# A graph-layer kernel on one core: the running sums of two batches overlapped, five tables instead of four, set-up issued in another order, and a new list of step times

## The chip, the core and the metric

The kernel runs on one core of one Trainium2 chip. The metric is the device time in microseconds (us) of one execution. Before the change three runs took 2403.47, 2404.86 and 2407.35 us, a median of 2404.86 us.

The engines have short names in the profile: PE is TensorE (matmuls; PEld is its weight load), DVE is VectorE, ACT is ScalarE, POOL is GpSimd, SP is SyncE, which here only issues transfers. Each of them takes its instructions in the order in which the program lists them.

## The reference

`x` holds 32 batches of 512 channels by 1024 nodes, `adj` is 512 by 512. There are two layers, each a normalisation over the nodes, a relu, and a graph operation that is added to `x`:

```python
# layer 0: attention over the nodes
h = relu(layernorm(x))
q, k = einsum('c,bcn->bn', wq, h), einsum('c,bcn->bn', wk, h)
scores = q[:, None, :] + k[:, :, None]
scores = where(scores > 0, scores, 0.01 * scores)
att = softmax(scores, axis=-1)                    # 1024 x 1024 a batch
agg = einsum('bcn,bmn->bcm', h, att)
x = x + relu(einsum('oc,bcm->bom', adj, agg) + bm[None, :, None])
# layer 1: a product with the squared adjacency
h = relu(layernorm(x))
x = x + einsum('bnf,nm->bmf', h, adj * adj) + bias
```

A score depends on one number of the row and one of the column. So the attention needs no 1024 by 1024 matrix: with the nodes sorted by `q`, each output row is a combination of a prefix sum and a suffix sum of the sorted value rows, read at the row where the sign of the score changes.

## The kernel before

**What a batch passes through.** The functions below are the steps of one batch, in the order of the data; PE's instructions for each are given.

- `load` brings the four 128 by 1024 pieces of `x` in, `stats` (DVE), `norm` (ACT: square root), `slopes` (DVE) and `relu` (ACT) make `h` from them. Layer 0 and layer 1 use the same functions (`stats0`, `stats1` and so on in the list of times).
- `scores` makes `q` and `k` on PE (tile `pq`), copies them out on ACT (`qr`), and sends them through memory (`qd`) into a row on all partitions, `qrow`. `columns` turns them into columns (`pr`, `qk`).
- `value` makes the 1024 value rows, eight tiles `pv` of eight matmul instructions; `spread` copies each to SBUF on ACT (tile `v`).
- `rank` counts on DVE how many `q` are smaller (eight columns of nodes); `lower` finds on ACT where the score changes sign. `to_rows`, `factors` and `from_rows` turn both into row numbers and factors on DVE.
- `scatter` writes the value rows on POOL's queue to their sorted places in a table in DRAM, `td`. There are `TABLES` of these, used in turn by the batches.
- `fetch` reads the sorted rows back (tiles `vs`, three a batch, from a pool of five), `weights` (ACT), `later` (DVE), `totals` (PE, tile `pd`) and `stationary` (POOL, tile `sm`) make the triangular matrices for the sums.
- `scan` is a chain of nine links. Each multiplies one block of the prefix sum and one of the suffix sum, 64 columns each (PE, tile `sc`, four instructions). `sums` copies its last row on ACT into the first row of the next block (L522, L523), so that the next link can start, then copies the block (L525, L526) and sends it to the table.
- `gather` reads each node's row of sums with eight indirect transfers on POOL's queue (tile `g`), `excess` and `divide` (DVE, with an exponential on ACT), `weigh` (ACT) and `combine` (DVE) put them together, and `turn` transposes the result on PE (tile `tr`) and adds it on DVE to a second copy of `x`, which `reload` brought (tiles `y`).
- `propagate` is layer 1's product: eight tiles `pg` of eight matmul instructions. `finish` (DVE) adds it and sends a piece of the output.

**What sets the order.** Nothing is scheduled by need. `PLAN` gives each step a time within its batch. Batch `b` adds `b * T`; the first and the last five batches are shifted by `FIRST` and `LAST`. All steps are sorted by that time and issued in that order:

```python
for n, t in enumerate(times):
    t = s.b * T + t + shift + stretch * (t - mean)
    steps.append((t, len(steps), f, (s, *lead, *(args[n] if args else (n,)))))
```

So the times are only an order, one for all engines; what an engine does at a moment follows from its own list and from its waits. PE's eight PSUM banks (`bank`) are handed out in the order of release. A tile that finds its bank still in use makes PE wait for the ACT or DVE instruction that empties it.

**One period.** In the middle of the run PE's list for a period is `scores` of batch b, its eight `value` tiles, the nine links of batch b-1, the eight `propagate` tiles of b-3 and the `turn` of b-2. Nearly every link stands alone between two tiles of 512 columns.

**Set-up.** Ahead of all steps the adjacency is loaded on SP's queue, then vectors on ACT's queue, masks are made on POOL and DVE, sixteen transfers of `pad` rows go out on ACT's queue (L260, L261), the adjacency is transposed on PE (L267) and copied by DVE (L268), and squared on POOL.

Of the kernel before, what the change touches and what calls it, by code (L numbers as in the profile page):

```python
# [16 lines left out]
P = 128  # L17
# [8 lines left out]
TABLES = 4  # L26
PLAN = {
    "columns": (1.84,),
    "combine": (
        214.04, 217.22, 206.24, 213.22, 203.06, 204.85, 202.37, 208.83, 220.2,  # L30
        221.83, 210.28, 216.32, 220.61, 221.9, 203.97, 206.56,
    ),
    "divide": (197.69,),
    "excess": (192.58,),
    "factors": (26.85,),
    "fetch": (67.06,),
    "finish": (275.07, 275.57, 281.48, 295.03, 317.93, 325.21, 315.57, 329.77),
    "from_rows": (68.15,),
    "gather": (160.21, 160.88, 169.39, 162.65, 163, 180.52, 164.85, 177.34),
    "later": (80.96,),  # L40
    "lift": (262.58, 269.88, 268.88, 273.93),
    "load": (-129.22, -82.94, -100.13, -53.61),
    "lower": (19.51, 17.67, 17.14, 24.76, 5.02, 13.05, 20.96, 48.33),
    "norm0": (-19.68,),
    "norm1": (240.99,),
    "propagate": (259.13, 265.4, 277.44, 283.36, 299.38, 300.5, 305.97, 309.52),
    "rank": (10.11, 17.8, 19.14, 5.65, 29.55, 35.11, 29.97, 33.03),
    "reload": (206.53, 195.2, 186.44, 204.89),
    "relu0": (-13.28, -12.83, -12.78, -11.68),
    "relu1": (248.39, 248.69, 248.95, 251.18),  # L50
    "scan": (86.07, 89.94, 103.3, 112.5, 121.08, 133.74, 140.67, 149.41, 151.56),
    "scatter": (40.11, 33.33, 32.57, 31.18, 51.68, 50.03, 50.02, 50.12),
    "scores": (-3.28,),
    "slopes0": (-19.05,),
    "slopes1": (244.13,),
    "spread": (14.21, 19.99, 13.53, 9.98, 24.66, 40.56, 35.96, 32.13),
    "stationary": (82.64, 96.64, 117.94),
    "stats0": (-76.58, -67.19, -75.23, -31.79),
    "stats1": (234.63, 235.11, 239.07, 234.96),
    "sums": (86.61, 100.16, 109.91, 113.65, 123.33, 138.82, 142.68, 150.09, 152.34),  # L60
    "to_rows": (27.23, 39.48),
    "totals": (84.47,),
    "turn0": (224.81, 225, 224.25, 224.65),
    "turn1": (229.2, 229.61, 229.06, 228.65),
    "value": (1.31, 6.43, 2.58, -2.04, 12.64, 17.61, 9.29, 13.53),
    "weigh": (211.43, 203.12, 199.8, 199.59, 214.55, 207.84, 213.35, 199.85),
    "weights": (77.29,),
}
FIRST = {
    "columns": ((10.25, 0), (-8.88, 0), (-1.28, 0), (-0.35, 0), (-4.55, 0)),  # L70
    "combine": ((0.76, -0.179), (2.86, -0.007), (1.11, -0.052), (2.15, 0.315), (3.85, -0.295)),
    "divide": ((-2.63, 0), (-3.76, 0), (1.77, 0), (-5.55, 0), (5.22, 0)),
    "excess": ((-1.4, 0), (-1.74, 0), (0.78, 0), (-1.88, 0), (-0.04, 0)),
    "factors": ((-1.65, 0), (0.24, 0), (-11.11, 0), (20.41, 0), (5.22, 0)),
    "fetch": ((1.66, 0), (1.42, 0), (0.16, 0), (2.7, 0), (2.46, 0)),
    "finish": ((7.67, -0.035), (-1.07, -0.048), (-1.08, -0.19), (1.65, 0.072), (7.11, -0.138)),
    "from_rows": ((-7.36, 0), (5.32, 0), (0.41, 0), (-11.13, 0), (1.83, 0)),
    "gather": ((2.03, -0.347), (6.25, 0.095), (6.91, -0.157), (4.86, 0.109), (-0.48, -0.141)),
    "later": ((0.59, 0), (-0.89, 0), (0.46, 0), (-1.56, 0), (-1.25, 0)),
    "lift": ((2.63, 0.053), (-2.39, -0.028), (-8.8, -0.373), (4.29, -0.574), (-5.63, -0.61)),  # L80
    "load": ((-4.06, 0.422), (-19.27, 0.242), (-9.74, -0.1), (-43.08, -0.218), (3.83, -0.041)),
    "lower": ((10.06, 0.047), (-2.11, 0.029), (0, 0.006), (-1.47, -0.638), (-0.64, -0.541)),
    "norm0": ((-0.28, 0), (-7, 0), (-16.93, 0), (-5.48, 0), (-7.56, 0)),
    "norm1": ((-2.89, 0), (-2.28, 0), (5.13, 0), (-4.22, 0), (4.28, 0)),
    "propagate": ((-0.51, -0.089), (-2.12, 0.048), (-0.37, -0.024), (0.9, -0.087), (0.8, -0.134)),
    "rank": ((12.28, 0.08), (-2.69, 0.063), (-1.25, -0.191), (-2.72, -0.187), (3.67, 0.356)),
    "reload": ((13.1, -0.159), (1.05, 0.07), (0.55, -0.006), (5.79, -0.056), (6.93, 0.28)),
    "relu0": ((4.04, -0.722), (-9.03, 0.1), (0.87, 0.055), (-1.74, 0.026), (-4.5, -0.079)),
    "relu1": ((-6.02, -0.262), (3.93, 0.189), (0.12, 0.08), (-6.68, -0.3), (5.36, -0.097)),
    "scan": ((-3.08, 0.008), (0.76, 0.008), (0.29, 0.01), (4.39, 0.049), (0.02, 0.004)),  # L90
    "scatter": ((9.9, -0.497), (-2.67, -0.18), (-1.41, -0.166), (13.52, 0.471), (-0.96, -0.009)),
    "scores": ((11.05, 0), (-7.18, 0), (-1.43, 0), (-1.1, 0), (-5.18, 0)),
    "slopes0": ((5.94, 0), (-4.02, 0), (-4.68, 0), (-4.91, 0), (-5.3, 0)),
    "slopes1": ((-4.88, 0), (-3.92, 0), (2.98, 0), (-6.44, 0), (6.4, 0)),
    "spread": ((15.49, -0.014), (-8.28, 0.055), (-1.18, 0.339), (5.11, -0.246), (-4.18, -0.13)),
    "stationary": ((-0.45, 0.012), (-3.58, -0.066), (2.3, 0.037), (3.72, 0.043), (0.11, 0.066)),
    "stats0": ((-4.41, 0.092), (-1.09, -0.037), (-11.92, -0.19), (-11.74, 0.144), (-4.6, 0.06)),
    "stats1": ((-4.42, -0.05), (-0.78, -0.165), (-2.4, -0.195), (-1.72, -0.801), (-0.4, -0.191)),
    "sums": ((-1.59, 0.008), (1.44, 0.008), (0.8, 0.011), (4.47, 0.048), (0.33, 0.004)),
    "to_rows": ((10.45, -0.184), (-1.39, -0.051), (-3.95, 0.188), (-5.12, -0.008), (3.22, 0.411)),  # L100
    "totals": ((-0.39, 0), (-1.31, 0), (2.21, 0), (3.78, 0), (-0.88, 0)),
    "turn0": ((-2.67, -0.147), (0.79, 0.144), (0.98, 0.006), (-1.5, -0.73), (2.76, -0.161)),
    "turn1": ((-5.71, 0.295), (-0.45, 0.083), (1.67, -0.222), (0.23, -0.077), (1.24, 1.019)),
    "value": ((12.84, -0.049), (-4.18, -0.108), (-0.34, -0.035), (-1.68, 0.56), (-0.83, -0.076)),
    "weigh": ((3.71, -0.151), (-4.8, 0.011), (2.02, 0.13), (-3.07, 0.09), (4.7, 0.116)),
    "weights": ((3.98, 0), (-0.18, 0), (3.93, 0), (-5.45, 0), (-0.47, 0)),
}
LAST = {
    "columns": ((-0.38, 0), (3.24, 0), (0.03, 0), (-4.32, 0), (-5.95, 0)),
    "combine": ((-13.52, -0.583), (-7.79, -0.661), (2.57, 0.018), (5.39, 0.14), (1.5, -0.058)),  # L110
    "divide": ((-17.36, 0), (-2.76, 0), (-0.77, 0), (1.72, 0), (-5.29, 0)),
    "excess": ((-15.23, 0), (-5.2, 0), (-2.78, 0), (5.24, 0), (-2.45, 0)),
    "factors": ((-2.1, 0), (-19.01, 0), (38.03, 0), (-13.91, 0), (0.21, 0)),
    "fetch": ((3.7, 0), (-1.79, 0), (-2.6, 0), (2.41, 0), (-10.36, 0)),
    "finish": ((37.02, -0.24), (-20.28, -0.179), (-0.12, 0.054), (7.26, 0), (7.17, 0.076)),
    "from_rows": ((-5.28, 0), (-0.46, 0), (19.09, 0), (10.28, 0), (-5.76, 0)),
    "gather": ((-7.27, -0.089), (-1.57, 0.275), (14.67, -0.488), (6.08, 0.503), (-1.65, 0.527)),
    "later": ((-2.82, 0), (-3.64, 0), (-2.12, 0), (1.08, 0), (-9.77, 0)),
    "lift": ((-33.59, -0.326), (-26.78, 0.49), (-1.54, 0.547), (5.74, 0.408), (-8.25, -0.218)),
    "load": ((0.07, 0.087), (2.75, -0.35), (4.99, -0.213), (-6.16, 0.111), (-0.4, -0.03)),  # L120
    "lower": ((-2.66, -0.306), (11.93, 0.06), (2.85, -0.242), (9.18, -0.176), (-3.11, 0.105)),
    "norm0": ((-8.11, 0), (-9.42, 0), (-8.14, 0), (-18.6, 0), (-2.96, 0)),
    "norm1": ((-25.17, 0), (-15.22, 0), (8.43, 0), (4.77, 0), (3.62, 0)),
    "propagate": (
        (-30.65, -0.512), (-18.28, -0.071), (-2.12, -0.017), (6.79, -0.024), (0.98, -0.118),
    ),
    "rank": ((-1.62, -0.025), (0.93, -0.001), (1.88, -0.179), (-4.5, 0.134), (-5.28, 0.009)),
    "reload": ((-20.37, -0.165), (5.3, 0.015), (4.48, 0.302), (2.59, -0.107), (7.99, -0.179)),
    "relu0": ((-0.04, 0.046), (3.05, 0), (1.47, -0.143), (-0.13, -0.026), (-2.37, 0.467)),
    "relu1": ((-21.92, -0.142), (-17.67, -0.206), (5.39, -0.385), (9.69, 0.26), (1.51, 0.12)),  # L130
# [22 lines left out]
def kernel(  # L153
# [104 lines left out]
    for td in tds:  # L258
        for o in range(2):
            nc.scalar.dma_start(sorted_rows(td, 0, NB)[o, 0], pad[0:NB, :])  # L260
            nc.scalar.dma_start(sorted_rows(td, NB - 1, 1)[o, :, 0], pad[0:HP, :])  # L261
# [401 lines left out]
```

## Time and profile before

| what | value |
|---|---|
| runs | 2403.47, 2404.86, 2407.35 us |
| the profiled execution | 2408.7 us, of it the span of instructions 2406.7 us |
| busy: PE, DVE, ACT, POOL | 2330.6, 1930.8, 1589.9, 687.6 us |
| share of the span: PE, DVE, ACT, POOL | 97%, 80%, 66%, 29% |
| transfers | 643.17 MB, mean 267 GB/s |
| mean granted clock of TensorE | 0.987 |

A page of the profile comes from one execution. Busy time is the time in which an engine executed; matmuls are pipelined, so that the mean duration of one (602 ns) is longer than the distance between two. A row of the timeline gives the start, the length and, in brackets, how long the engine had been idle and what ended that. The slices of the page cut the span in 40 equal parts.

### The profile page before, as it was taken

How to read it: one execution, taken by the hardware profiler on the slowest of the kernel's cores; microseconds unless marked ns; L12 is line 12 of the kernel's file. 1: busy time of each engine (PE TensorE's matmuls, PEld its weight loads, DVE VectorE, ACT ScalarE, POOL GpSimd, SP SyncE). 2: the span in 40 equal slices, each digit the busy share in tenths (PEclk: the TensorE clock that was granted, in tenths of full speed). 3: DMA queues.
4: the chain of work that ended last, by engine and by line, in shares of the span. 5: the costliest groups of instructions: out<-in, count | busy, mean ns of one | idle time of the engine just before them, and what ended most of it. 6: DMA issues, size and time to landing. Idle time of an engine off the chain costs nothing.

```text
span 2406.7 us, 28301 instructions
## 1 busy us (share of the span) xinstructions
PE 2330.6 (97%) x7632; PEld 981.1 (41%) x7632; DVE 1930.8 (80%) x5012; ACT 1589.9 (66%) x2873; POOL 687.6 (29%) x973
## 2 busy tenths in 40 slices
PE   6889999999999999999999999999999999999898
PEld 2233444443444444444444444444344444444333
DVE  6568788888888898888898888888888878787765
ACT  3667667577676677667677667677767666757551
POOL 1233233223222223322323322323323223323310
PEclk9889999999999999999999999999999999999999
DMA  5689889898888898899898899889889888788882
GB/s 169 176 280 288 273 261 313 250 278 294 272 296 282 248 293 288 270 294 286 258 274 292 275 284 292 270 259 293 282 280 295 238 263 288 260 283 267 263 268 95
DMA packets 206718, 643.17 MB, mean 267 GB/s; under 512 B 29080, under 2 KB 29208, under 8 KB 206560
## 3 DMA queue, kind: packets, MB, share of 16 engines
q1 hardware_dynamic: 146704, 370.65, 54.5%
q0 software_dynamic: 57344, 268.99, 29.2%
q10 hardware_dynamic: 2512, 1.73, 0.3%
q8 instruction: 62, 1.02, 0.2%
q14 instruction: 96, 0.79, 0.1%
HBM read 429.94 MB, written 211.32 MB: 266 GB/s over the span
## 4 chain that ended last, share of the span: by engine, by line
PE 82%; DMA 5%; DVE 5%; ACT 3%; issue 2%; POOL 1%; SPq 1%; ACTq 0%; POOLq 0%; DVEq 0%
PE pg L577 33%; PE pv L429 31%; PE sc L512 11%; PE tr L570 4%; PE pq L326 2%; DMA vs<-td 1%; DMA td<-v,idx 1%; DMA qd<-qr 1%; DVE junk L371 1%; DVE st L296 1%; DVE g L563 1%; DMA qrow<-qd 1%; DVE junk L366 1%; ACT g L559 1%; POOL td L442 1%
## 5 line engine op out<-in xcount | busy, mean ns | idle before, releaser
L577 PE MATMUL pg<-h,wsq 128*128 128x512 f32 x2048 | 937.1, 602 | 7.7 <-ACT h L314 7.7
L429 PE MATMUL pv<-wmT,x 128*128 128x512 f32 x2048 | 910.8, 598 | 0.8 <-DVE y L585 0.8
L577 PEld LDWEIGHTS pg<-h,wsq 128*128 128x128 f32 x2048 | 374.4, 191 | 525.7 <-issue 495.2
L429 PEld LDWEIGHTS pv<-wmT,x 128*128 128x128 f32 x2048 | 379.8, 190 | 493.4 <-issue 458.3
L534 POOL DMA_INDIRECT g<-td,idg x256 | 247.7, 967 | 755.2 <-DMA qd<-qr 248.2
L442 POOL DMA_INDIRECT td<-v,idx x256 | 272.1, 1063 | 572.6 <-ACT vs L523 208.2
L522 ACT COPY vs<-sc 1x512 f32<-1x512 f32 x256 | 146.0, 570 | 388.4 <-PE sc L512 375.9
L512 PE MATMUL sc<-vs,sm 128*64 128x512 f32 x1152 | 332.2, 629 | 28.3 <-ACT vs L522 17.2
L382 ACT ACTIVATE junk<-qrow,qk 128x1024 bf16<-128x1024 f32 x256 | 294.0, 1148 | 91.6 <-DVE qk L345 47.6
L563 DVE SCALAR_TENSOR_TENSOR g<-g,cf 128x512 f32<-128x512 f32 x512 | 348.3, 742 | 4.9 <-ACT g L559 4.6
L585 DVE SCALAR_TENSOR_TENSOR y<-pg,bm_sb,y 128x512 f32<-128x512 f32 x256 | 186.0, 738 | 77.1 <-PE pg L577 75.6
L572 DVE SCALAR_TENSOR_TENSOR y<-tr,nbm,y 128x512 f32<-128x512 f32 x256 | 176.9, 744 | 62.1 <-PE tr L570 57.8
L525 ACT COPY t<-sc 128x512 f32<-128x512 f32 x288 | 168.8, 586 | 84.0 <-PE sc L512 65.8
L371 DVE TENSOR_SCALAR_CACHE_REDUCE junk<-qrow,qk,cnt 128x640 bf16<-128x640 f32 (+6 forms) x224 | 180.4, 805 | 8.2
L366 DVE TENSOR_SCALAR_CACHE_REDUCE junk<-qrow,qk 128x384 bf16<-128x384 f32 (+6 forms) x224 | 165.2, 737 | 19.6 <-DMA qrow<-qd 12.2
L559 ACT ACTIVATE g<-g,cf 128x512 f32<-128x512 f32 x256 | 169.6, 717 | 3.1 <-DVE cf L553 2.9
L296 DVE BATCH_NORM_STATS2 st<-x 128x6 f32<-128x512 f32 x256 | 162.7, 676 | 0.0
L296 DVE BATCH_NORM_STATS2 st<-y 128x6 f32<-128x512 f32 x256 | 160.2, 668 | 0.0
L320 DVE TENSOR_TENSOR y<-y,bias_sb 128x1024 f32<-128x1024 f32 x128 | 155.6, 1225 | 5.6 <-ACT h L314 5.5
L436 ACT COPY v<-pv 128x512 f32<-128x512 f32 x256 | 144.3, 578 | 20.1 <-PE pv L429 13.8
L314 ACT ACTIVATE x<-x,nmr,rstd 128x1024 f32<-128x1024 f32 x128 | 148.5, 1232 | 9.6 <-DVE nmr L307 9.6
L512 PEld LDWEIGHTS sc<-vs,sm 128*64 128x64 f32 x1152 | 63.7, 137 | 220.2 <-issue 96.7
(107 smaller groups left out, 1815.5 us busy)
## 6 DMA issues: line engine op xcount, KB each, us to landing
vs<-td SPq DMA_DIRECT2D x192, 384.8 KB
td<-t SPq DMA_DIRECT2D x576, 128.2 KB
x<-in_x_dram SPq DMA_DIRECT2D x128, 512.0 KB
y<-in_x_dram SPq DMA_DIRECT2D x128, 512.0 KB
out_dram<-y SPq DMA_DIRECT2D x128, 512.0 KB
qrow<-qd SPq DMA_DIRECT2D x32, 512.0 KB
td<-v,idx POOLq DMA_INDIRECT x256
g<-td,idg POOLq DMA_INDIRECT x256
```

The lines of the kernel that those rows point to most:

```text
L296: nc.vector.bn_stats(st[:, i, :], s.x[c][:, ts(i, HALF)])
L366: nc.vector.tensor_scalar(junk[:, 0 : j * P], s.qrow[:, 0 : j * P], qc, None, ALU.is_le, ALU.add, accum_out=s.cnt[:, 0, j : j + 1],)
L371: nc.vector.tensor_scalar(junk[:, j * P :], s.qrow[:, j * P :], qc, first, ALU.is_lt, ALU.add, accum_out=s.cnt[:, 1, j : j + 1],)
L382: nc.scalar.activation(junk, s.qrow, AF.Sign, bias=s.qk[:, 1, j : j + 1], accum_out=s.sgn[:, j : j + 1])
L429: nc.tensor.matmul(pv, s.h[c][:, ts(j, P)], wmT[:, c, :], start=(c == 0), stop=(c == NC - 1))
L442: i = nc.gpsimd.indirect_dma_start(tds[s.b % TABLES][:, :], bass.IndirectOffsetOnAxis(ap=s.idx[j // 4][:, j % 4 : j % 4 + 1], axis=0), v[: ...
L512: nc.tensor.matmul(p[ts(k, HP), :], s.sm[i][k], s.vs[h][:, 0:C], start=True, stop=True)
L534: nc.gpsimd.indirect_dma_start(s.g[:, j, :], None, tds[s.b % TABLES][0 : 3 * NB * HP, :].rearrange("(s k) w -> s (k w)", k=3), bass.Indire ...
L559: nc.scalar.mul(r, r, s.cf[:, 0, j : j + 1])
L563: nc.vector.scalar_tensor_tensor(r, s.g[:, j, k * W : k * W + C], s.cf[:, k, j : j + 1], r, ALU.mult, ALU.add)
L577: nc.tensor.matmul(pg, wsq[:, r, ts(c, P)], s.h[r][:, ts(i, HALF)], start=(r == 0), stop=(r == NC - 1),)
L585: nc.vector.scalar_tensor_tensor(xh, s.pg.pop((c, i)), bm_sb[:, c : c + 1], xh, ALU.add, ALU.add)
```

## The change

Three things change.

- **The steps' times.** All of `PLAN`, `FIRST` and `LAST` is new, and `T` is 80.54 instead of 79.84. The nine links of a batch are spread over nearly two periods. In the middle of the run PE's list for a period becomes: `scores` of b, three `value` tiles, `totals` and link 0 of b-1, link 6 of b-2, link 1 of b-1, five `value` tiles, link 7 of b-2, link 2 of b-1, three `propagate` tiles of b-4, link 3 of b-1, link 8 of b-2, two `propagate` tiles, link 4 of b-1, and the rest of `propagate` around the `turn` of b-3, then link 5 of b-1. So the second half of a batch (gather to finish) comes one period later than before.
- **Five tables.** `TABLES` is 5, and three small tiles that live longer have one buffer more.
- **Set-up as steps.** Only the identity, `wqk` and the epsilon stay ahead of the steps, with a square root of one column that loads ACT's table. The rest becomes seven steps with times of their own. Three pieces of `x` are asked for ahead of the adjacency; its copies out of PSUM go from DVE to ACT, behind the first four relus; the pads (now 20) and the two vectors `bm` and `bias` go to SP's queue, behind the first `qrow`; the squaring on POOL stands between two scatters.

```diff
-TABLES = 4
+TABLES = 5
 PLAN = {
...
-    "scan": (86.07, 89.94, 103.3, 112.5, 121.08, 133.74, 140.67, 149.41, 151.56),
+    "scan": (90.31, 96.47, 108.29, 124.9, 142.06, 153.31, 174.19, 187.88, 206.23),
...
-    "sums": (86.61, 100.16, 109.91, 113.65, 123.33, 138.82, 142.68, 150.09, 152.34),
+    "sums": (91.26, 100.33, 117.83, 130.05, 147.14, 161.48, 177.9, 193.73, 222.2),
...
-    adjn = gp.tile([P, NC, C], F32, tag="G", name="adjn")
-    nc.sync.dma_start(adjn, adj.rearrange("(r p) c -> p r c", p=P))
+    ident = const.tile([P, P], F32, name="ident")
+    make_identity(nc, ident)
...
+    root = const.tile([P, 1], F32, name="root")
+    nc.scalar.activation(root, eps_sb, AF.Sqrt)
...
-    for td in tds:
-        for o in range(2):
-            nc.scalar.dma_start(sorted_rows(td, 0, NB)[o, 0], pad[0:NB, :])
-            nc.scalar.dma_start(sorted_rows(td, NB - 1, 1)[o, :, 0], pad[0:HP, :])
...
-        nc.vector.tensor_copy(wmT[:, c, :], pt)
...
+    def adjacency(s):
+        s.adj = gp.tile([P, NC, C], F32, tag="G", name="adjn")
+        nc.sync.dma_start(s.adj, adj.rearrange("(r p) c -> p r c", p=P))
+
+    def turn_adjacency(s):
+        for c in range(NC):
+            pt = bank(f"pt_{c}")
+            for o in range(NC):
+                nc.tensor.transpose(pt[:, ts(o, P)], s.adj[:, o, ts(c, P)], ident)
+            nc.scalar.copy(wmT[:, c, :], pt)
+
+    def square(s):
+        nc.gpsimd.tensor_tensor(wsq, s.adj, s.adj, ALU.mult)
+
+    def biases(s):
+        nc.sync.dma_start(bm_sb, bm.rearrange("(c p) -> p c", p=P))
+        nc.sync.dma_start(bias_sb, bias.partition_broadcast(P))
+        nc.vector.tensor_scalar(nbm, bm_sb, -1.0, None, ALU.mult)
+
+    def pads(s):
+        pad = vp.tile([P, W], F32, tag="v", name="pad")
+        nc.vector.memset(pad, 0.0)
+        nc.vector.memset(pad[:, C : C + 1], FAR)
+        for td in tds:
+            for o in range(2):
+                nc.sync.dma_start(sorted_rows(td, 0, NB)[o, 0], pad[0:NB, :])
+                nc.sync.dma_start(sorted_rows(td, NB - 1, 1)[o, :, 0], pad[0:HP, :])
...
-        s.B = sp.tile([P, NN], F32, tag="B", name=f"B_{s.b}", bufs=5)
+        s.B = sp.tile([P, NN], F32, tag="B", name=f"B_{s.b}", bufs=6)
...
-        s.idg = sp.tile([P, NN], U32, tag="idg", name=f"idg_{s.b}", bufs=4)
+        s.idg = sp.tile([P, NN], U32, tag="idg", name=f"idg_{s.b}", bufs=5)
...
-        s.arg = sp.tile([P, 2, NN], F32, tag="arg", name=f"arg_{s.b}", bufs=4)
+        s.arg = sp.tile([P, 2, NN], F32, tag="arg", name=f"arg_{s.b}", bufs=5)
...
-    T = 79.84
+    T = 80.54
...
+        if b == 0:
+            for f in (
+                adjacency, turn_adjacency, square, biases, pads, compare_mask, masks,
+            ):
+                plan(s, f, f.__name__, args=((),))
```

The steps `compare_mask` and `masks` hold the mask code that stood ahead, unchanged. PE has the same 7632 instructions in both kernels' work, in another order.

## Prediction

> **What bounds the kernel now.** I read the busy times first, then the slices, the chain of waits, the busy times by stage, and last PE's timeline at the places where it idles.
>
> ```profile
> PE 2330.6 (97%) x7632; PEld 981.1 (41%) x7632; DVE 1930.8 (80%) x5012; ACT 1589.9 (66%) x2873; POOL 687.6 (29%) x973
> PE   6889999999999999999999999999999999999898
> PEclk9889999999999999999999999999999999999999
> PE 82%; DMA 5%; DVE 5%; ACT 3%; issue 2%; POOL 1%; SPq 1%; ACTq 0%; POOLq 0%; DVEq 0%
> ```
>
> PE is busy nearly throughout; gaps and a lower clock stand only in the first four slices and near the end. The stages (start:end, length, then busy time of PE, PEld, DVE, ACT, POOL, granted clock, DMA share, GB/s) say the same in microseconds:
>
> ```profile
> 100.00:200.00 100.00, 81.61 (x286) 31.40 (x285) 64.20 (x199) 72.14 (x138) 33.74 (x49) 0.86 0.83 255
> ...
> 1000.00:1500.00 500.00, 500.00 (x1665) 210.83 (x1664) 418.52 (x1086) 348.14 (x629) 146.00 (x210) 1.00 0.88 279
> ...
> 2200.00:2300.00 100.00, 89.80 (x279) 36.32 (x278) 69.75 (x174) 58.75 (x113) 35.05 (x44) 0.93 0.85 272
> ```
>
> In the middle PE never waits, and DVE is at 418.52/500 = 84%. The first `pq` of each batch marks the periods:
>
> ```profile
> 687.03 1.93 PE L326 MATMUL pq<-x,wqk 128*32 128x256 f32 x32
> ```
>
> The next ones start at 758.60 and 830.17: 71.57 us each, and the timeline shows this exactly for 17 periods, 615.46 to 1832.14. So three things can change the time: PE's own time for a period, the lost time at the start, and that at the end. The start in PE's rows (start, length, in brackets the idle time before and its releaser):
>
> ```profile
> 27.25 4.48 PE L326 MATMUL pq<-x,wqk 128*32 128x256 f32 x32 [16.75 <-ACT x L314]
> ...
> 172.46 2.54 PE L512 MATMUL sc<-vs,sm 128*64 128x512 f32 x4 [6.01 <-ACT vs L522]
> ```
>
> Its cause stands in ACT's row, a table load behind the `pad` transfers:
>
> ```profile
> 23.92 1.28 ACT L301 ACT_TABLE_LOAD   x1 [23.92 <-DMA td<-pad]
> ```
>
> By such rows `pq` of batch 9 starts 615.46 us in, with 547 us of work for PE before it: 68 us lost. The end: `pq` of batch 31 starts at 2199.93, PE's last product ends at 2402.2, with 173 us of work between: 29.3 lost.
>
> ```profile
> 2314.36 1.67 PE L512 MATMUL sc<-vs,sm 128*64 128x512 f32 x4 [0.66 <-ACT vs L522]
> ...
> 2355.89 3.94 PE L570 MATMUL tr<-ident,g 128*128 128x128 f32 x32
> 2359.84 7.13 PE L577 MATMUL pg<-h,wsq 128*128 128x512 f32 x16
> 2371.70 3.78 PE L577 MATMUL pg<-h,wsq 128*128 128x512 f32 x4 [4.74 <-ACT h L314]
> ```
>
> **What the Trainium skill says.** "TensorE: Matmul & The Clock Gate", Part 1 (the HAM clock gate): after an idle window of about 3.4 us the clock halves, and about 3.4 us of work restore it. The trace agrees in kind: after 6.01 us idle a link takes 2.54 us instead of 1.08; 2.59 us (at 1978) were already enough. The same page says that ACT's and VectorE's queues are strictly in order; the 23.92 us above agree. "TensorEngine Tiling (Array Packing)", Key Properties: "Mode switching requires drain". A link uses half the columns; the trace agrees with a price:
>
> ```profile
> 1009.14 1.08 PE L512 MATMUL sc<-vs,sm 128*64 128x512 f32 x4
> 1010.15 3.70 PE L577 MATMUL pg<-h,wsq 128*128 128x512 f32 x8
> 1013.78 1.08 PE L512 MATMUL sc<-vs,sm 128*64 128x512 f32 x4
> ```
>
> Link to link is 4.64 us, the tile between takes 3.48 (24 value instructions take 10.45), so a lone link costs 1.16. A 512-column pass costs .435, the link's two pairs .87: .29 is switching.
>
> **Part 1, the middle.** No instruction is added, so the price is in the order. Nine groups of links a period become five ({0, 6, 1}, {7, 2}, {3, 8}, 4, 5): four merges at .2 to .25 (most of .29) save .8 to 1.0. Added: link 1 needs the row that `sums` copies after link 0. Where links followed each other dependently the distance was 2.34 (2312.02 to 2314.36); link 6 fills one slot, and with `totals` and the first matmul's part the hole is about .4. Net -.4 to -.6, so 71.0 to 71.2; I take a quarter off for merges that save less, -.35. PE's other waits, by row durations counted from the period's `pq`:
> - Link 3 is wanted at 46.2. Its row is made by sum 2, queued on ACT behind sum 7 and behind the exponential of `excess`, which waits for DVE, whose eight ranks end first: about 40.9, then .72 + 2 x 1.77 for the ACT steps. Slack 2.0.
> - Sum 3 before link 4: slack 3.
> - The fetch of the third `vs` takes a buffer that link 5 of two batches back frees; landing and `weights`, `later`, `stationary` end near 10.3, wanted at 12.7: slack 2.4.
> - Every PSUM bank is freed earlier than wanted. POOL is at 29%, SP only issues; five tables let the scatter of b run while gathers of b-3 wait.
>
> At nothing: the longer-lived tiles, which hold no engine, and the transfers: bytes for a period are the same (DMA share .88 before), and those that move by a period are hidden as long as the slacks above hold. Bounds: -.8 (all merges whole, no hole) to +.6 (no merge gain, hole doubled): over 26 periods -21 to +16, value **-9**.
>
> **Part 2, the start.** Removed from ACT's queue: 16 pads (13.09 to 23.92) and two vectors; the table load lies under x's loads. Loads, at 375 GB/s with three pieces ahead, end near 12.5; `pq` 0 can start at about 16, -11. The four transposed copies on ACT (.48 each) end before `qr`, at about 21.7 against 31.8: -10. SP's new order: `qd`, `qrow` (1.7 between), then 20 pads (at about .65, 13) and `bm`, `bias`, then later loads. `nbm` on DVE therefore waits until about 54, and behind it in DVE's list stand `slopes` of batch 1, for which ACT's relus and then PE's `pq` wait: PE idle about 51 to 57, 6 lost. The fifth table's four pads are in these 13 us. The two mask steps lie on POOL and DVE while PE does value tiles. `square` (3.6 us on POOL) delays four scatters under ranks that are later anyway. Walking on: `pq` 3 at about 156 against 184.54. Then link 3 of batch 2 waits for a sum that stands on ACT behind an exponential of batch 3 and behind `excess` of batch 0, both waiting for DVE after eight ranks: idle about 9, 3.6 and 7. So `pq` 5 at 288.5 against 323.25, 34.75 earlier; but a batch's `propagate` (27.9) and its `turn` and links (5.8) are then still owed: gain 1. Bounds: -15 (ranks earlier than walked, no such idles) to +10 (fetches behind the pads late as well). Value **-1**.
>
> **Part 3, batches 26 to 31.** Before, these five periods took 367.8, 10 more than 5 x 71.57. The new list keeps the merged order into the last batch: half of it comes back, **-5** (-10 to +5).
>
> **Part 4, the drain.** The links of batch 31 lie among eight `propagate` tiles of batch 28, so few holes like .66 remain; `turn` and `propagate` of 29 and 30 follow with work beside them. But all of `propagate` 30 stands ahead of `turn` 31, and nothing is left between it and `propagate` 31. The distance of these was 15.8 (2355.89 to 2371.70), 7.1 of it filled and 4.74 idle; now about 11 are idle, and the clock rule above costs about 3 more: +9 there. Of the other 24.5 of the 29.3 lost, named idles are 10.2 (5.57, 2.03, 1.29, .67, .66); the rest is half clock behind them and small gaps. I take 20 of the 24.5 as filled. Value **-11** (-18: all filled, and a hole of 9; +5: three quarters stay).
>
> **Sum.** -9 - 1 - 5 - 11 = -26 on the profiled execution's 2408.7: 2382.7. That execution is 3.8 above the median of 2404.86; between a proportional shift (2379) and none of it (2382.7) I take **2381**.
>
> **Rivals.**
> - *The ring over DVE and ACT* (slower). Slack 2.0 at link 3 rests on durations at 84% DVE load. If excess on DVE ends later than walked, PE waits each period: 26 us for each us beyond 2.0, and the merge gain of 9 vanishes in the stall. At 3 us late 2381 + 26 + 9 = 2416; it turns the sign from 2.8 us on. For it: in the first slices L522 itself is late, and PE's 6.01 us above ended on it. Against: the middle has 16% of DVE free.
> - *The deeper pipeline gives it back.* Merges bring nothing (+9) and start or drain lose what they gain (+10): 2397 to 2409. For it: one batch more is filled and emptied.
> - *Links side by side don't get cheaper*, PE still drains for each: part 1 is the hole alone, +.4 x 26 = 10 instead of -9: 2400. Against: `pd` beside `sc` adds only .13.
>
> **How the numbers follow.** About 0.2%, 4.8 us, is what a measurement can tell. Forecast .58, its own range 2362 to 2398 (parts at two thirds of their bounds). Ring .20, of which nearly all is slower. Given back .14: half within 4.8 us, a fifth slower, the rest faster. No cheaper links .08, half faster. Sum: faster .66, same .11, slower .23. Range 2362 to 2418: a tenth lies above (ring over 3 us), a tenth below.
>
> **What would show it.** In the profile after (PE lines move by 18: links L530, `propagate` L595, `turn` L588): `pq` 71.2 apart between 700 and 1800, with no idle over .5 before L530; first `pq` near 16; an idle of about 9 before an L530 near 200; about 11 us of idle before the last L595. Wrong if the period is above 71.6, if L530 waits on <-ACT in each period, or if the middle is right and the ends aren't.

## The result and the profile after

The changed kernel takes 2404.13 us (median of 12 runs, 2400.07 to 2409.92) against 2403.52 for the kernel before (12 runs, 2395.8 to 2407.35): a ratio of 1.0006, interval 0.9994 to 1.0017. Executed again on another chip, where both kernels were some 8 to 12 us longer, it had 2416.61 against 2411.86: 1.0020, 1.0012 to 1.0027. So it is the same time or 0.2% more; 2381 had been forecast. The two profiled executions mislead here: 2400.17 us after against 2408.7 before looks like a gain, but one is 4 us below its kernel's median of twelve runs, the other 5 above.

The page of the profile after, in the order in which that of before was read: busy times, PE's slices, its clock, the shares of the chain that ended last.

```profile
PE 2305.7 (96%) x7632; PEld 1004.9 (42%) x7632; DVE 1936.4 (81%) x5008; ACT 1585.2 (66%) x2880; POOL 723.7 (30%) x973
...
PE   5787999999999999999999999999999999999897
...
PEclk9898999999999999999999999999999999999999
...
PE 87%; DMA 6%; DVE 2%; ACT 2%; issue 1%; SPq 1%; POOL 1%; POOLq 0%; DVEq 0%; ACTq 0%
```

The middle is as full as before; the first slices have more gaps, not fewer. By stage (start:end, length, busy PE, PEld, DVE, ACT, POOL, clock, DMA share, GB/s):

```profile
0.00:100.00 100.00, 65.37 (x216) 28.69 (x217) 52.66 (x182) 44.92 (x78) 20.20 (x39) 0.90 0.56 163
100.00:200.00 100.00, 89.54 (x289) 34.34 (x288) 57.05 (x192) 67.98 (x134) 28.10 (x45) 0.95 0.77 226
200.00:300.00 100.00, 83.23 (x254) 36.52 (x253) 78.09 (x211) 69.75 (x131) 35.20 (x50) 0.86 0.85 263
...
1000.00:1500.00 500.00, 500.00 (x1675) 217.84 (x1673) 424.07 (x1099) 349.62 (x637) 158.08 (x210) 1.00 0.87 282
```

For the middle the busy share tells nothing (500 of 500 in both kernels); the distance from one batch's `pq` to the next one's does:

```profile
1019.71 1.93 PE L344 MATMUL pq<-x,wqk 128*32 128x256 f32 x32
...
1090.64 1.93 PE L344 MATMUL pq<-x,wqk 128*32 128x256 f32 x32
```

That is 70.93 us, exact for 17 periods, where 71.57 were needed before.

**Where the time went.** Each kernel was profiled twice. The starts of `pq` 5 and `pq` 31 cut the span in three. (`pq` 5 is the first `pq` instruction of batch 5.) At `pq` 5 the changed kernel still owes 33.7 us of PE's work that the other has done, at `pq` 31 37.0 (64 matmuls of 512 columns at .435, 52 transposes at .11, 12 link instructions at .29, by the counts in the traces). With means over the two profiles:

| stretch | before | after | change, less the work moved | predicted |
|---|---|---|---|---|
| to `pq` 5 | 323.25, 325.07 | 307.59, 313.84 | -13.4 + 33.7 = +20.3 | -1 |
| `pq` 5 to `pq` 31 | 1876.68, 1873.23 | 1849.81, 1849.82 | -25.1 + 3.3 = -21.8 | -9 - 5 |
| `pq` 31 to the end | 206.77, 204.57 | 241.07, 250.89 | +40.3 - 37.0 = +3.3 | -11 |
| span | 2406.7, 2402.9 | 2398.5, 2414.6 | +1.8 | -26 |

The middle gained more than forecast, and the start took nearly all of it. Paired the other ways, the two profiles of each kernel put the start between +16 and +24 and the end between -3 and +9, so the end's +3.3 is not clear of the spread; with the mean of the five ends given below, 247.4, it is +4.7. The second profile of the kernel before (2404.87 us) also lies below all 49 runs of that kernel on its chip (2407.0 to 2417.47), so a sum of +1.8 says no more than the medians do. From batch 9 to batch 26 the period repeats to a hundredth of a microsecond, but for one or two longer ones in some executions; what differs between executions of one kernel lies ahead of that, in the last five periods and in the end.

### The profile page after: what moved, and what is told of

Same layout as the page of the kernel before. It is cut to its first block, busy times and chain, and to the rows that moved or that the text cites. A ratio compares the mean times of both kernels' runs of the same rounds, so it can differ in the third digit from the quotient of the medians.

```text
span 2398.5 us, 28425 instructions
## 1 busy us (share of the span) xinstructions
PE 2305.7 (96%) x7632; PEld 1004.9 (42%) x7632; DVE 1936.4 (81%) x5008; ACT 1585.2 (66%) x2880; POOL 723.7 (30%) x973
## 3 DMA queue, kind: packets, MB, share of 16 engines
q0 software_dynamic: 57344, 268.99, 30.0%
## 4 chain that ended last, share of the span: by engine, by line
PE 87%; DMA 6%; DVE 2%; ACT 2%; issue 1%; SPq 1%; POOL 1%; POOLq 0%; DVEq 0%; ACTq 0%
PE pg L595 35%; PE pv L447 34%; PE sc L530 12%; PE tr L588 4%; DMA vs<-td 2%; PE pq L344 2%; DVE g L581 1%; DMA td<-pad 1%; DMA x<-in_x_dram 1%; DMA g<-td,idg 1%; DMA qd<-qr 0%; POOL g L552 0%; ACT junk L400 0%; SPq L477 0%; ACT t L543 0%
## 5 line engine op out<-in xcount | busy, mean ns | idle before, releaser
L595 PE MATMUL pg<-h,wsq 128*128 128x512 f32 x2048 | 913.3, 598 | 10.6 <-ACT h L332 10.6
L520 POOL TENSOR_TENSOR sm<-mask_a,wc 128x192 f32<-128x192 f32 x96 | 49.4, 515 | 1283.8 <-DVE wc L497 815.5
L530 PE MATMUL sc<-vs,sm 128*64 128x512 f32 x1152 | 322.8, 629 | 38.7 <-POOL sm L520 17.2
L460 POOL DMA_INDIRECT td<-v,idx x256 | 292.3, 1142 | 146.8 <-POOL v L459 49.8
L389 DVE TENSOR_SCALAR_CACHE_REDUCE junk<-qrow,qk,cnt 128x896 bf16<-128x896 f32 (+6 forms) x224 | 180.3, 805 | 8.2
L384 DVE TENSOR_SCALAR_CACHE_REDUCE junk<-qrow,qk 128x128 bf16<-128x128 f32 (+6 forms) x224 | 165.5, 739 | 14.0 <-DMA qrow<-qd 9.2
L530 PEld LDWEIGHTS sc<-vs,sm 128*64 128x64 f32 x1152 | 77.3, 139 | 231.9 <-issue 90.4
L577 ACT ACTIVATE g<-g,cf 128x512 f32<-128x512 f32 x256 | 163.5, 712 | 6.4 <-DVE cf L571 6.4
```

Source lines behind the costliest of these rows:

```text
L389: nc.vector.tensor_scalar(junk[:, j * P :], s.qrow[:, j * P :], qc, first, ALU.is_lt, ALU.add, accum_out=s.cnt[:, 1, j : j + 1],)
L460: i = nc.gpsimd.indirect_dma_start(tds[s.b % TABLES][:, :], bass.IndirectOffsetOnAxis(ap=s.idx[j // 4][:, j % 4 : j % 4 + 1], axis=0), v[: ...
L530: nc.tensor.matmul(p[ts(k, HP), :], s.sm[i][k], s.vs[h][:, 0:C], start=True, stop=True)
L595: nc.tensor.matmul(pg, wsq[:, r, ts(c, P)], s.h[r][:, ts(i, HALF)], start=(r == 0), stop=(r == NC - 1),)
```

## The experiments

All are edits of the changed kernel. A ratio is to the kernel before on the same chip, with its interval. "End" is the stretch from `pq` 31 to the end of the span. Where single steps were moved, a dictionary gives them another time in the list, and nothing else is changed (its entries are shown shortened below):

```diff
             t = s.b * T + t + shift + stretch * (t - mean)
+            t = MOVED.get((name, s.b, n), t)
```

**The two kernels once more.** No edit.

> The changed kernel, unaltered, executed again. The first pair of profiles stood 8.5 us apart, the medians of twelve runs +0.6 us. Theory A: single executions differ in the start, where transfers and waits race, and in the end; the period in the middle repeats to the hundredth, 70.93 us, and the span lies anywhere from 2398 to 2408. Rival: the period itself differs between executions (70.9 to 71.3), and the comparison of 17 periods in two profiles is not to be trusted. Ratio to the kernel before 0.999 to 1.002.

> The kernel before, unaltered, executed again. Theory A: period 71.57 us again, span 2398 to 2407, and what differs from the first profile (2406.7) lies before the pq of batch 9 (615.46) or after that of batch 26. Rival: the period differs.

Periods 70.93 and 71.57 again. `pq` 5 was at 313.84 instead of 307.59, and the end took 250.89 us instead of 241.07. Together with three later kernels in which the list of the end is untouched (bias_first, pads_by_table, tables4) it took 241.1 to 250.9 us, mean 247.4. The span alone therefore can't show an edit worth 5 us; the stretch that it touches can.

### The start

The timeline of the profile after has SP's issues of the first and last pad and of the fetch, DVE's wait and PE's:

```profile
34.02 0.31 SPq L267 DMA_DIRECT2D td<-pad  x1
...
59.83 0.45 SPq L268 DMA_DIRECT2D td<-pad  x1
...
63.27 4.64 SPq L477 DMA_DIRECT2D vs<-td  x6
...
66.44 0.17 DVE L259 TENSOR_SCALAR nbm<-bm_sb 128x4 f32<-128x4 f32 x1 [19.68 <-DMA bm_sb<-in_L_gnn_bm_dram]
...
69.60 6.20 PE L447 MATMUL pv<-wmT,x 128*128 128x512 f32 x8 [19.81 <-ACT x L332]
```

The waits of SP's queue in this stretch (total us, times, longest):

```profile
SPq L268 <- DMA td<-pad: 15.7, 10, 2.1
```

Twenty pads take SP from 34.0 to 60.3: 1.31 us each, because every second one waits for the landing of the one ahead, ten times, 15.7 us in all. In the kernel before, ACT's queue had them in fours:

```profile
13.09 1.60 ACTq L260 DMA_DIRECT2D td<-pad  x4
16.89 2.45 ACTq L261 DMA_DIRECT2D td<-pad  x4
19.37 1.61 ACTq L260 DMA_DIRECT2D td<-pad  x4
21.49 2.40 ACTq L261 DMA_DIRECT2D td<-pad  x4
```

Four go out, then the four that come second for the same tables. Sixteen pads had only two pauses, of 2.2 and .5 us, and took .68 us each. So the price of a pad differs with its place in the list; the grouping by fours on SP's queue was not tried. Only behind the pads come loads of `x`, `bm` and the fetch of batch 0. Two edits ask which of these counts.

```diff
-    "biases": (44.64,),
+    "biases": (30.0,),
```

> The changed kernel with the step biases (bm, bias and nbm) issued ahead of the pads instead of behind them. The prediction's theory (only the wait for nbm counts): PE's idle 19.81 us before the value tiles of batch 1 goes and nothing takes its place, 13 to 19 us faster than the changed kernel. Rival (the pads hold SP's queue for 26 us, and everything behind them is late): nbm is in time and pq of batch 1 starts about 20 us earlier, but the fetch of batch 0 is still issued at about 63, link 0 still starts at 84 to 85, PE waits there for 17 to 20 us, and the time is the changed kernel's within 3 us.

2416.12 us, 1.0016 (1.0006 to 1.0025), with 2416.61 for the unaltered kernel on the same chip. `pq` of batch 1 came 16 us earlier (59.70), and the idle time moved to link 0:

```profile
82.32 2.43 PE L530 MATMUL sc<-vs,sm 128*64 128x512 f32 x4 [13.40 <-POOL sm L520]
```

`pq` of batch 2 was where it had been (118.75; before that edit 118.87 and 119.34). The wait that the prediction named was the first of two in a row, and taking it away alone gains nothing.

```diff
+    "pads": ((0, 0), (-30, 0), (-30, 0), (-30, 0), (-30, 0)),
...
-        for td in tds:
-            for o in range(2):
+        td = tds[s.b]
+        for o in range(2):
...
+        if b < TABLES:
+            plan(s, pads, "pads", args=((),))
```

> The changed kernel with the four pads of a table issued with the batch that uses the table first (batch 0: where all twenty stood; batches 1 to 4: early in the batch). SP's queue at the start is shorter by sixteen pads, about 21 us. Theory that the pads on SP's queue are the loss: bm lands near 46, the fetch of batch 0 is issued when its scatters have landed (about 59 instead of 63.3), loads of batch 2 about 20 us earlier; link 0 at 76 to 80 instead of 84.9; PE's idle up to link 0 falls from 20 to 10 to 13; 5 to 12 us faster than the changed kernel. Theory that only nbm counts: 13 to 19 us faster. Theory that the start is bound by the scatters and the fetch in any case: within 3 us.

2409.39 us, 0.9989 (0.9982 to 0.9996), 7.2 us less than the unaltered kernel on that chip. The fetch was issued at 59.41, link 0 started at 74.07 behind 5.09 us of idle time, and `pq` 9 at 589.35. In the ten profiles whose list is unaltered up to there it is at 593.49 to 599.66, mean 595.1. So the pads on SP's queue cost 5.8 us by `pq` 9 and 7.2 by the time, about a third of the start's 20.

```diff
-TABLES = 5
+TABLES = 4
```

> The changed kernel with four tables instead of five, so sixteen pads. Theory (in the new list the gathers of a batch are all issued before the scatters three batches on, so that the fifth table carries nothing, and costs four pads of 1.31 us on SP's queue): period 70.93, the start 3 to 6 us shorter by pq of batch 9, time 0 to 6 us less. Rival (the scatters wait for the gathers of the batch that had the table): period over 71.2 or idle time at links in every period, and slower.

2401.14 us, 0.9998 (0.9988 to 1.0007); period 70.93, `pq` 9 at 589.74. The fifth table carries nothing in the middle and costs its pads at the start. Four pads fewer start `pq` 9 as early as sixteen fewer did (589.35), in one profile each, so from there on something else seems to bind the start.

The rest of the start can be read from the profiles. PE's idle times of over .3 us up to `pq` 5 sum to 61.2 and 67.1 us, in the kernel before to 45.9 and 48.4; in the first of them the 19.81 above and, at links behind 200 us, 6.35, 1.69, 4.86 and 3.86 us are the largest since the first instruction. Around these four the granted clock was 0.50 (start:end, length, busy PE, clock, DMA share, GB/s):

```profile
207.41:227.89 20.48, 12.19 (x32) 0.50 0.97 277
244.96:251.78 6.82, 5.51 (x20) 0.50 0.69 211
```

PE worked 17.7 us in these stretches; at half the clock half of it, 8.9 us, is lost (an estimate). No edit took these waits away.

### The middle

In a period of the changed kernel PE's rows are, from `totals` on (start, length; x4 is one link), with ACT's two copies of the last row of link 0 (the PE rows first):

```profile
1032.54 3.49 PE L530 MATMUL sc<-vs,sm 128*64 128x512 f32 x12
1035.96 17.43 PE L447 MATMUL pv<-wmT,x 128*128 128x512 f32 x40
1053.33 1.94 PE L530 MATMUL sc<-vs,sm 128*64 128x512 f32 x8
1055.20 10.57 PE L595 MATMUL pg<-h,wsq 128*128 128x512 f32 x24
1065.69 1.94 PE L530 MATMUL sc<-vs,sm 128*64 128x512 f32 x8
...
1033.73 0.58 ACT L540 COPY vs<-sc 1x512 f32<-1x512 f32 x1 [5.19 <-PE sc L530]
1034.33 0.58 ACT L541 COPY vs<-sc 1x512 f32<-1x512 f32 x1
```

A pair of links takes 1.87 to the next start and some .1 more in the tile behind it, .35 less than two lone ones at 1.16. The triple of links 0, 6 and 1 takes 3.42 + .1, as much as three lone ones: its own saving, twice .35, is eaten by a wait for link 0's row, though no idle time is shown. The single instructions show it: the two halves of link 1 (prefix and suffix) start at 1034.36 and 1034.96, each .05 us behind the end of its copy on ACT, where the halves of links 0 and 6 start .01 apart.

```diff
-    "scan": (90.31, 96.47, 108.29, 124.9, 142.06, 153.31, 174.19, 187.88, 206.23),
+    "scan": (90.31, 96.9, 108.29, 124.9, 142.06, 153.31, 174.19, 187.88, 206.23),
```

> The changed kernel with link 1 one value tile later, so that links 0 and 6 stand as a pair and link 1 alone. In the profile a pair costs 1.87 plus about .1, a lone link 1.16, the triple 3.42 plus .1. Theory (the triple holds a hidden wait of about .5 us for the row of link 0, shown by no idle time): period 70.93 - .37 = 70.5 to 70.6 us, 9 us over the run. Rival (three links side by side save two switches and there is no wait): one switch more, period 71.1 to 71.3.

2399.80 us, 0.9985 (0.9976 to 0.9995). The period is 70.57 us, .36 less. The rows show the pair, a tile, and link 1 alone:

```profile
1026.51 1.92 PE L530 MATMUL sc<-vs,sm 128*64 128x512 f32 x8
1028.37 3.70 PE L447 MATMUL pv<-wmT,x 128*128 128x512 f32 x8
1032.00 1.08 PE L530 MATMUL sc<-vs,sm 128*64 128x512 f32 x4
```

The other way round:

```diff
-    "scan": (90.31, 96.47, 108.29, 124.9, 142.06, 153.31, 174.19, 187.88, 206.23),
+    "scan": (90.31, 96.47, 109.2, 124.9, 142.06, 153.31, 174.19, 187.88, 208.1),
```

> The changed kernel with its two pairs of links split: link 2 one propagate tile behind link 7, link 8 one behind link 3. Theory (a pair of links costs 1.87 + about .1 where two lone ones cost 2 x 1.16, so .35 a pair, and this is the whole gain of the middle): period 70.93 + .70 = 71.6 us, the period of the kernel before (71.57). Rival (the gain comes from something else, such as the turn in two pieces instead of three): under 71.2.

The undisturbed period was 71.63, .06 from that of the kernel before: the two pairs are the whole gain of the steady period. Some periods were longer (71.9 to 76.2), with idle times of .3 to 1.4 us at links and `totals`; why is open. The one execution took 2430.58 us; the price of a pair is read from the undisturbed periods.

### The end

The profile after, at the last fetch (SP), its third tile (ACT), the links behind it and the last products (PE):

```profile
2218.00 3.93 SPq L477 DMA_DIRECT2D vs<-td  x6
2220.55 0.98 POOL L552 DMA_INDIRECT g<-td,idg  x1 [9.50 <-PE tr L588]
2237.40 0.30 ACT L486 ACTIVATE w<-vs,nq 128x3 f32<-128x3 f32 x1 [6.41 <-DMA vs<-td]
2239.61 4.27 PE L530 MATMUL sc<-vs,sm 128*64 128x512 f32 x7 [9.03 <-POOL sm L520]
...
2308.39 41.47 PE L595 MATMUL pg<-h,wsq 128*128 128x512 f32 x96
2349.70 3.66 PE L588 MATMUL tr<-ident,g 128*128 128x128 f32 x32
2363.94 29.76 PE L595 MATMUL pg<-h,wsq 128*128 128x512 f32 x64 [10.59 <-ACT h L332]
```

The last line is as predicted. The idle time of 9.03 us ahead of link 6 of batch 30, called the hole below (16.95 in the second profile), was not: ACT first used the third tile of the fetch 19.4 and 25.2 us after the fetch was issued, where in the kernel before it was 13.5 for the fetch of batch 0 and 16.5 for the last one:

```profile
2261.88 4.08 SPq L459 DMA_DIRECT2D vs<-td  x6
...
2278.42 0.30 ACT L468 ACTIVATE w<-vs,nq 128x3 f32<-128x3 f32 x1 [5.67 <-DMA vs<-td]
```

The gathers of batch 29 go out from 2 us behind the fetch on.

```diff
+    ("gather", 29, 0..7): 31 * T + 93.2,      # behind stationary 31
```

> The changed kernel with the eight gathers of batch 29 put behind the first stationary step of batch 31 on POOL's queue. In four profiles of this order they start 2 us after the fetch of batch 31 is issued, and the third tile of that fetch is used 19.4 to 25.2 us after the issue. Theory (the fetch is slow because the gathers share the DMA engines with it): alone, the third tile is used 12 to 16 us after the issue and PE's hole ahead of link 6 of batch 30 falls from 9 to 18 us to 3 to 6; the turn of batch 29 then comes later than before, so that the time need not fall. Rival (the fetch waits for its own scatters or for SP's queue, not for bandwidth): 19 to 25 us again and the same hole.

The third tile was used 13.65 us after the issue (2220.29 to 2233.94), the hole was 4.67, and the end took 253.5: new idle times of 9.86 and 2.92 us stood at later links. So the fetch is slow because of the gathers beside it, and holding them back only moves the wait.

```diff
+    ("weights", 31, 0): 31 * T + 91.71,       # behind relu1 of batch 28
+    ("later", 31, 0): 31 * T + 92.08,
+    ("propagate", 28, 0..2): 31 * T + 92.6,   # ahead of link 6 of batch 30
```

> The changed kernel with two things near the end reordered: on ACT the relus of layer 1 of batch 28 come ahead of the weights of batch 31 (which wait for the fetch), and on PE the first three propagate tiles of batch 28 come ahead of link 6 of batch 30 and link 0 of batch 31. Theory (PE's hole of 9 to 18 us there is a queue in the wrong order: ACT stands at the fetch while the relus are ready): the hole falls to 3 to 7, the stretch from pq of batch 31 to the end from 241 to 251 (four profiles) to 235 to 241, time 6 to 10 us less. Rival (the chain of links of batch 31 sets the end, tiles are only fillers): the hole goes, but 10 us of new idles appear between later links or ahead of the last products, and the time is the same.

2405.28 us, 1.0009 (1.0000 to 1.0018); end 241.3. The hole was filled, but 3.82 us of idle time came at a link of batch 31, which now follows the one ahead with no tile between, and 12.37 us ahead of the last product, as the rival has it.

```diff
+    ("scan", 31, 8): 31 * T + 203.9, ("sums", 31, 8): 31 * T + 204.0,
+    ("turn1", "turn0", "stats1", "norm1", "slopes1", "relu1", 31): 31 * T + 381 to 385,
```

> The changed kernel with link 8 and sum 8 of batch 31 two propagate tiles earlier, and its turn, statistics, norm, slopes and relus ahead of the last three propagate tiles of batch 30 (and of their finish steps). Theory (the last idle of 10.4 to 10.9 us and the half clock behind it come from having nothing left between the turn and the last product): the idle ahead of the last product falls to under 2, its duration from 29.8 to 28, the stretch from pq of batch 31 to the end by 9 to 12 us. Rival (the chain from link 8 over sums, gather and excess to the turn sets the end): the turn starts only 7 us earlier with PE idle ahead of it, and 3 to 7 us are gained.

2405.12 us, 1.0010 (0.9998 to 1.0023); end 247.3, with a hole of 16.79. From the third tile to the end it took 159.5 us instead of 161.1 and 161.4. The last 10.6 us went, but the turn waited 4.74 and 2.21 us for `combine`, as its rival has it.

Both edits, two `stationary` steps earlier, and links 1 to 8 of batch 31 closer together:

```diff
+    ("scan", 31, 1..5): 31 * T + 101.4 to 122,   # before: 104.0 to 162.3
+    ("scan", 31, 6..8): 31 * T + 148.0 to 158,   # before: 183.7 to 216.5; sums behind each
+    ("propagate", 28, 4..5): 31 * T + 145 to 146,
```

> The changed kernel with the end reordered in three ways at once: as in drain_a (three propagate tiles of batch 28 and its relus ahead of what waits for the last fetch), links 1 to 8 of batch 31 closer together, and as in tail (its turn and what follows ahead of the last three tiles of batch 30). Theory (in six profiles the end comes 161 to 162 us after the third tile of the last fetch is used, wherever that falls, against 127 to 128 in the kernel before: links spread between tiles make that chain, drain_a and tail alone each leave it as it is): this distance falls to 142 to 150, the stretch from pq of batch 31 to the end from 241 to 251 to 226 to 236, time 10 to 16 us less. Rival (the end is bound by PE's work and by the landing of the fetch): distance 155 or more, time within 5 us.

2418.32 us, 1.0070 (1.0053 to 1.0088); end 255.7. Worse: turn 29 started 38.6 us behind the third tile of the fetch instead of 28.7, and the gathers of batches 30 and 31 followed it 39 us apart (2289.89 and 2329.01). This suggested the turns, not the links, as the chain. Then came three edits on top of each other: one on what holds turn 29 (its eighth gather stands behind `stationary` 31 on POOL), that with drain_a, and that with tail too.

```diff
+    ("gather", 29, 2): 31 * T + 92.95,        # ahead of stationary 31
```

> The changed kernel with one gather of batch 29, the eighth, moved ahead of the stationary step of batch 31 on POOL's queue. Theory (two things bind side by side at the end: the chain over the one buffer of gathered rows, which hangs on this gather, and PE's work, which is without idle from the hole to the last turn): turn 29 comes 8 to 20 us earlier, but the hole and the last idle stay and the stretch from pq of batch 31 to the end stays at 241 to 251. Rival (the chain alone binds): stretch 8 to 15 us shorter.

> eighth_gather and drain_a together: three propagate tiles of batch 28 fill PE's hole, and the chain no longer hangs on the fetch. drain_a alone had the stretch at 241.3, with idles of 3.8 and 12.4 further on. Theory (drain_a was held by the chain): those idles fall to under 1 and about 10.6, stretch 232 to 238. Rival (something else holds the chain): 240 or more.

> eighth_a and tail together (the last turn and what follows ahead of the last three tiles of batch 30). Theory (with hole and chain gone, the last idle of 10.6 and the half clock behind it are all that is left to take): no idle over 4 us behind the fetch, stretch 222 to 230, time 12 to 20 us less than the changed kernel, ratio to the kernel before .992 to .996. Rival: 236 or more.

Ends of 244.7, 245.2 and 244.8; eighth_gather took 2405.96 us (1.0013, 1.0004 to 1.0021), eighth_a 2406.42 in its one execution, eighth_a_tail 2402.52 (0.9997, 0.9986 to 1.0008). The gather was issued early (2229.5), yet turn 29 came no earlier in eighth_gather (2273 against 2269 and 2285), with the hole at 11.77: the guess falls, and so does the expectation of the two built on it. On DVE `later` 31 waited for the fetch too, ahead of `excess` 29. That was moved last:

```diff
+    ("lift", 28), ("finish", 27), ("from_rows", 31), ("excess", 29), ("divide", 29): 31 * T + 91.6 to 91.67,
+    ("weigh", 29), ("combine", 29): 31 * T + 92.12 to 92.36,   # right behind later 31
+    ("gather", 29, 2), ("gather", 29, 4): 31 * T + 91.1 to 91.2,
```

> eighth_a_tail with the steps of batch 29 taken from behind the last fetch on all three queues: on DVE the four lifts of batch 28, three finish steps of batch 27, from_rows of batch 31, excess and divide of batch 29 ahead of later of batch 31 and combine of batch 29 right behind it, on ACT weigh of batch 29 right behind the weights of batch 31, on POOL all gathers of batch 29 ahead of the stationary step. Theory (the place behind the fetch's third tile on DVE's queue holds the chain of turns): combine of batch 29 is done 12 to 16 us earlier against the third tile, turns 30 and 31 follow 35 to 38 us apart as before, the distance from the third tile to the end falls from 156 to 160 to 140 to 148, the stretch from pq of batch 31 to the end to 226 to 234. Rival (links of batch 31, which now come up to 5 us later, or PE's work bind): distance over 152.

2413.16 us, 1.0043 (1.0029 to 1.0057); end 253.8. The theory falls too, and the row of DVE says why: `excess` now waits for the gathered rows themselves. The `weights` of batch 31 stand behind its exponential on ACT, so that the third tile was used 35.2 us after the fetch was issued and the hole was 13.86.

```profile
2253.26 0.17 DVE L624 TENSOR_TENSOR cf<-g,arg 128x8 f32<-128x8 f32 x1 [11.83 <-DMA g<-td,idg]
```

The gathers, issued up to 2232, landed at 2253. One gather moves 788 KB (268.99 MB of the indirect queue in before's page, less 256 scatters of 263 KB, by 256), eight 6.3 MB; the fetch is 2.4 MB. In the changed kernel the DMA engines are 97% busy there:

```profile
2205.00:2250.00 45.00, 35.60 (x115) 16.58 (x115) 31.57 (x63) 26.90 (x51) 15.75 (x19) 0.89 0.97 306
```

From the third tile of the last fetch to the end it is 161.1 and 161.4 us, against 128.3 and 127.1 in the kernel before: 33.6 more. PE's work accounts for it. Behind that tile PE has 256 matmuls of `propagate` instead of 192, 96 transposes instead of 64 and 48 link instructions instead of 36: 34.8 us more at the prices above. From the end of the hole to the last turn (2239.61 to 2353.4) PE idles 2.1 us in all, in both profiles, so its list sets the pace there.

A second chain stands close behind PE's list. The rows gathered have one buffer (tile `g`), so the gathers of a batch start when the turn of the batch before has read them. POOL's rows of the changed kernel show the first gather of batches 30 and 31:

```profile
2271.03 0.97 POOL L552 DMA_INDIRECT g<-td,idg  x1 [17.25 <-DVE y L590]
...
2309.55 0.97 POOL L552 DMA_INDIRECT g<-td,idg  x1 [27.85 <-DVE y L590]
```

38.5 us apart (38.2 in the second profile). The changed kernel has three such rounds to go behind that tile (29, 30, 31), the kernel before two (30, 31). In tail, where PE comes to the last turn three tiles (10.4 us) earlier, the turn waits 7.0 us for `combine`, a step of this round. That both limits lie so close is a likely reason why each edit that eased one of them gained little; it was not tested by an edit: a second buffer for `g` was not tried.

### The parts together

> drain_all, pads_by_table and link1_apart in one kernel. If the three parts are as separate as the theory has them, the gains add: start 5 to 10 us, 20 periods by .36 us, drain 10 to 16: 22 to 33 us less than the changed kernel, a ratio of .987 to .992 to the kernel before. Rival (one of the parts is hidden by another): under 15 us.

2404.15 us, 1.0005 (0.9995 to 1.0016): `pq` 31 at 2141.83, 15.6 earlier than in the first profile after, and an end of 256.6, which gave it back: the drain of drain_all.

> eighth_a_tail, pads_by_table and link1_apart in one kernel. The three stretches are apart: start 5 to 10 us, 20 periods by .36, the end 12 to 20: 24 to 37 us less than the changed kernel, ratio .985 to .991 to the kernel before. Rival (an earlier part makes a later one worse, as the drain of best did): less than 15.

2390.45 us, 0.9954 (0.9940 to 0.9969): `pads_by_table`, `link1_apart` and eighth_a_tail. `pq` 31 at 2143.46, end 245.3. This is the fastest version, 0.46% (some 11 us) below the kernel before. The end lies inside the 241.1 to 250.9 of the untouched list, so the gain comes from start and middle.

> chain29 with pads_by_table and link1_apart. By the theory 10 to 14 us less than best2, which had a ratio of .9954 to the kernel before: .989 to .992. Rival: .994 or more.

2398.18 us, 0.9985 (0.9978 to 0.9991), end 254.8 against 253.8 of chain29 alone: its end costs here what it cost there.

## Why the prediction was wrong

**The middle was right in its mechanism, the size of two terms was off.** Forecast was a period of 71.0 to 71.2, and 71.2 after a discount; it is 70.93. A merged pair saves .35, not .2 to .25; the triple saves nothing, its wait being worth twice that, .7, and not .4. The slack at link 3 held: in the period from 1019.71 the copy that it waits for ends at 44.2 and link 3 starts at 46.0, counted from `pq`. So the ring over DVE and ACT, the rival for slower, did not bind.

**The start failed at the price of a pad.** The first `pq` at 16.30 and `qr` at 21.44 came as walked. But .65 us for a pad was taken from ACT's queue in the kernel before, where they stood in fours; on SP's queue it was 1.31, so `nbm` ran at 66.4 instead of 54 and PE idled 19.81 us instead of 6. The second failure is in kind: the walk followed `nbm` alone and counted the fetch of batch 0 behind the pads only in its bound, where the experiment shows it binding next. `pq` 3 came at 168.80 instead of 156, 12.8 late, about the 13.8 us by which that idle time is longer. From there to `pq` 5 (307.59 instead of 288.5) 6.3 more were lost. The idle times named for batch 2 (9, 3.6 and 7) were 6.35 with 1.69, 4.86 and 3.86, 2.8 less than forecast; the half clock around them, worth about 8.9, is not named in the walk, and the two together make 6.1. The start was 20.3 us longer, less the work moved. The pads explain about a third of it by experiment; the rest is read from one profile and was not tested.

**Batches 26 to 31 are part of the gain of the middle.** The five periods took 357.43 and 358.14 us instead of 367.79 and 365.26, 8.7 less where 5 had been forecast.

**The end failed at "few holes remain".** From `pq` 31 to the end of PE's last product 29.2 and 27.0 us were lost before, beside 173 of work; forecast were 18.3. The changed kernel lost 26.3 and 36.1 beside 210.0. The step that failed had 20 of 24.5 us of idle time filled. A hole of 9 to 17 us opened at the last fetch instead: its landing beside eight gathers, 19.4 and 25.2 us, had no place in the sum. The last idle time was forecast at 11 and is 10.59; the half clock behind it cost about 1.9 (29.76 for 64 matmuls at .435), not 3.

**The sum** lay 26 below a profiled execution that was itself 5 above its kernel's later median. The result lies inside the band of the rival "the deeper pipeline gives it back", but not by its mechanism, which had the merges bring nothing. Some sums of the prediction do not come out. The terms at link 3 (40.9 + .72 + 2 x 1.77) end at 45.2 and leave a slack of 1.0, not 2.0 (1.8 was measured). The terms beside the bounds of a period (four merges at .29, twice the hole of .4) give -1.2 and +.8, not -.8 and +.6. Two thirds of all bounds, counted from the median, give 2362 to 2429, not to 2398. None of these decided the error.

## What to carry to other kernels

In a full steady state, the distance of one repeated instruction is a gauge to a hundredth of a microsecond, and a change of order can be priced there; start and end need their own accounts, with the work that a deeper pipeline moves from one to the other. A price belongs to its place in the list and its neighbours: here a pad that waits for the one ahead took nearly twice, and a fetch beside gathers 1.4 to 1.9 times as long as the same step elsewhere. When one wait is taken out and nothing is gained, look for the next wait of the same cause before giving the cause up.

## What was not expected of the hardware

The clock: a link after 1.69 us of idle time already ran at half speed, while after 1.29 us one did not. The Trainium skill, "TensorE: Matmul & The Clock Gate", Part 1 (the HAM clock gate), has the clock halve after an idle window of about 3.4 us that runs freely. Here two shorter gaps in a row, with 1.08 us of work between them, were enough: the granted clock was 0.50 from 111.84 to 115.25 us.

```profile
109.21 1.08 PE L530 MATMUL sc<-vs,sm 128*64 128x512 f32 x4 [1.29 <-ACT vs L541]
111.98 2.57 PE L530 MATMUL sc<-vs,sm 128*64 128x512 f32 x4 [1.69 <-ACT vs L540]
```

A wait of half a link can be invisible: the triple of links shows no idle time, since one half runs while the other waits .60 us, and moving one link away made the period .36 us shorter.
